# A graph attention kernel on one core: a shared PSUM bank listed whole, and a sorted table of places in the place of a scheduler

## The chip, the core and the metric

The kernel runs on one NeuronCore of a Trainium2 chip. Its engines are TensorE (PE in the profile, with its weight loads as PEld), VectorE (DVE), ScalarE (ACT), GpSimd (POOL) and SyncE (SP); each works through its own list of instructions in order and waits on semaphores. SyncE issues most transfers, GpSimd those that add into SBUF. The metric is the device time of one execution in microseconds (us); a change is told by the median of several.

## The reference, cut to what matters

A batch of 32 graphs of 512 nodes goes through two graph attention layers, behind a layer norm and with a residual sum around:

```python
def gat_layer(x, mask, W, a_src, a_dst, bias, concat):
    B, N, _ = x.shape
    H, F = a_src.shape
    xl = (x @ W).reshape(B, N, H, F)
    asrc = jnp.einsum('bnhf,hf->bnh', xl, a_src)
    adst = jnp.einsum('bnhf,hf->bnh', xl, a_dst)
    e = jax.nn.leaky_relu(asrc[:, :, None, :] + adst[:, None, :, :], NEG_SLOPE)
    e = jnp.where(mask[..., None], e, NEG_INF)
    attn = jax.nn.softmax(e, axis=1)
    out = jnp.einsum('bsdh,bshf->bdhf', attn, xl)
    if concat:
        out = out.reshape(B, N, H * F)
    else:
        out = out.mean(axis=2)
    return out + bias
mask = (adj > 0) | jnp.eye(N, dtype=bool)[None]
h = jax.nn.elu(gat_layer(h, mask, W1, att_src1, att_dst1, b1, concat=True))
h = gat_layer(h, mask, W2, att_src2, att_dst2, b2, concat=False)
...
h = jnp.maximum(_layernorm(x, axis=-1), 0.0)
x = x + _L0_gnn_ref(adj, h, ...)
```

`x` is 32 x 512 x 512 in float32 and `adj` int32. The first layer has 4 heads of 256 (W1 is 512 x 1024), the second one head of 512 (W2 is 1024 x 512). A float32 matmul shows as two passes in the trace, so `x2` in a list of instructions is `x4` there.

## The kernel before, in words

The kernel is written as a list of jobs. `Program.add` takes an engine, a cost, the keys that the job reads, those that it writes, and a function that emits its instructions; keys give the dependencies, so a key that is listed as written makes the job wait for every reader of it before. The helpers `act`, `dve`, `dma` (SyncE), `accumulate` (GpSimd, a transfer that adds) and `pe` add jobs. Where they record an instruction the profile gives their own line: L531 is every product, L514 every ScalarE operation, L517 every VectorE one, L520 every transfer of SyncE.

Graphs run in a pipeline. After a prologue (graph 0 whole, the projection of graph 1), 31 turns follow. A turn holds the second half of the first layer of one graph (`gather1`), the projection of a graph ahead (`project1`), the second layer of one behind (`project2`, `gather2`) and the preparations of the next (`load`, `norm`, `masks`). Products are Strassen's seven half products (`sevens`), numbered 1 to 7.

In the projection the product numbered 5 (`SMALL = (5,)`) is done by seven smaller ones of 128 x 129 columns, in `step`: a small block. There are two blocks in each of the 31 projections. The small products 2 and 3 go to the banks where the results are summed. The five others share one PSUM bank `tk`: 5 writes its upper half, key `tk + (1,)`, and 1, 6, 7 and 4 its lower half, key `tk + (0,)`. They run as 5, 1, 2, 6, 3, 7, 4. ScalarE copies the first two out: `f<-mm 128x129` is the copy of 5, `mm<-mm 128x129` that of 1 (and later of 4). VectorE adds 6 and 7 with `f`. In the trace and in the order, 5 is the first `mm<-wx,hx` of a block, 1 the `mm<-w_sb,hs 128x129` into the same bank, 2 the one into another bank, 6 the second `mm<-wx,hx`, 3 `mm<-w_sb,hx`, 7 `mm<-w_sb,hs` again, 4 `mm<-wx,hs`.

The scores of the softmax are spread over the partitions in `Soft.spread`: a VectorE transpose (`as<-z`), a 4 KB transfer out (`das<-as`) and a transfer in that repeats the rows (`as<-das`); the row maxima go the same way (`rr<-low`, `drr<-rr`, `rr<-drr`). ScalarE then works on `as` (`l<-as,z`), VectorE takes masked maxima (`l<-l,mt`), and later `p<-rr,z` on VectorE, a transfer that adds the mask (`p<-dm`, on GpSimd's queue) and the exponential (`p<-p,z`) on ScalarE make the attention matrix. The residual is loaded by `t<-in_x_dram`, stored by `out_dram<-t`. For graphs 0 and 1 the normed rows are transposed by TensorE with an identity matrix (`mm<-identf,x`, copied out as `ht<-mm`), for all others by a transfer.

What sets each engine's order is `Program.order`: it plays the program through with the costs, with latencies between engines (`PAIRS`, `CROSS`, `SAME`) and a model of the two DMA queues (`KIND`, `wires`). Whenever an engine is free in that play, it takes the ready job with the lowest rank. A rank is `PLACES[v] / 100` plus the length of a turn for each turn since the first. The emission follows that play.

## Time and profile before

| what | value |
| --- | --- |
| median of 3 runs | 2773.44 us (2768.58 to 2775.35) |
| profiled execution | 2769.33 us |
| its span | 2767.6 us |
| granted TensorE clock, mean | 0.999 |
| TensorE busy | 2742.4 us, 99% |
| VectorE busy | 2558.2 us, 92% |
| ScalarE busy | 2229.1 us, 81% |
| DMA | 502.14 MB, mean 181 GB/s |
| first product | 12.06 us after the start |

The span is the time from the first to the last record of the core; the time of an execution is a little longer. Times in the timeline count from the span's start. A row of the timeline reads: start, duration, engine, line, operation, what it writes and reads, shape, count, and in brackets the idle time before it with what ended it. Durations of matmuls include about 0.16 us in which the next one already runs. In the windows, the first number behind an engine is its busy time there, and PEclk the clock that TensorE was granted.

### The profile page before, as it was taken

How to read it: one execution, taken by the hardware profiler on the slowest of the kernel's cores; microseconds unless marked ns; L12 is line 12 of the kernel's file. 1: busy time of each engine (PE TensorE's matmuls, PEld its weight loads, DVE VectorE, ACT ScalarE, POOL GpSimd, SP SyncE). 2: the span in 40 equal slices, each digit the busy share in tenths (PEclk: the TensorE clock that was granted, in tenths of full speed). 3: DMA queues.
4: the chain of work that ended last, by engine and by line, in shares of the span. 5: the costliest groups of instructions: out<-in, count | busy, mean ns of one | idle time of the engine just before them, and what ended most of it. 6: DMA issues, size and time to landing. Idle time of an engine off the chain costs nothing. (4 is left out here: it accounts for less than half of the span.)

```text
span 2767.6 us, 42320 instructions
## 1 busy us (share of the span) xinstructions
PE 2742.4 (99%) x12924; PEld 2371.8 (86%) x12924; DVE 2558.2 (92%) x6732; ACT 2229.1 (81%) x4907; POOL 313.1 (11%) x356
## 2 busy tenths in 40 slices
PE   7999999999999999999999999999999999999999
PEld 6788888888888888888888888888888888888887
DVE  8999999999999999999999999999999999999996
ACT  5978888778887788877888877888778788788883
POOL 0110111101111111111011111111111111101110
PEclk9999999999999999999999999999999999999999
DMA  8657766667666667667676766766676767767563
GB/s 232 176 157 182 203 167 184 187 176 194 182 183 179 182 176 196 178 175 195 173 201 172 182 187 178 192 186 180 180 188 175 201 167 180 195 165 208 162 171 112
DMA packets 375864, 502.14 MB, mean 181 GB/s; under 512 B 222804, under 2 KB 227668, under 8 KB 375636
## 3 DMA queue, kind: packets, MB, share of 16 engines
q1 hardware_dynamic: 329844, 332.68, 42.4%
q0 software_dynamic: 45792, 166.74, 25.1%
q8 instruction: 103, 1.69, 0.3%
q14 instruction: 125, 1.02, 0.1%
HBM read 316.41 MB, written 51.31 MB: 133 GB/s over the span
## 5 line engine op out<-in xcount | busy, mean ns | idle before, releaser
L531 PE MATMUL mm<-w_sb,hs 128*128 128x257 f32 (+3 forms) x2908 | 667.0, 367 | 5.1 <-ACT mm L514 3.3
L531 PEld LDWEIGHTS mm<-w_sb,hs 128*128 128x128 f32 x2908 | 539.7, 190 | 87.7 <-ACT mm L514 6.7
L525 POOL DMA_DIRECT2D p<-dm x314 | 273.2, 875 | 2295.0 <-DVE p L517 764.3
L531 PE MATMUL mm<-w_sb,ht 128*128 128x258 f32 x2112 | 528.6, 382 | 2.7 <-ACT mm L514 2.5
L531 PE MATMUL mm<-p,xl 128*128 128x258 f32 (+1 forms) x1984 | 495.8, 383 | 0.1
L531 PE MATMUL mm<-w_sb,h 128*128 128x257 f32 x2056 | 477.8, 379 | 0.0
L517 DVE SCALAR_TENSOR_TENSOR p<-rr,z 128x512 f32<-128x512 f32 (+1 forms) x636 | 456.0, 742 | 2.4 <-DMA rr<-drr 2.4
L531 PEld LDWEIGHTS mm<-w_sb,ht 128*128 128x128 f32 x2112 | 393.7, 190 | 63.6 <-ACT mm L514 6.4
L514 ACT ACTIVATE p<-p,z 128x512 f32<-128x512 f32 (+1 forms) x636 | 433.4, 720 | 17.7 <-DVE p L517 12.4
L531 PEld LDWEIGHTS mm<-w_sb,h 128*128 128x128 f32 x2056 | 389.0, 189 | 58.4 <-ACT xl L514 0.5
L531 PEld LDWEIGHTS mm<-p,xl 128*128 128x128 f32 x1984 | 367.2, 190 | 52.7 <-issue 6.0
L514 ACT ACTIVATE mm<-mm 128x257 f32<-128x257 f32 (+2 forms) x498 | 169.8, 347 | 269.2 <-PE mm L531 236.2
L514 ACT ACTIVATE l<-as,z 128x512 f32<-128x512 f32 x516 | 354.4, 716 | 30.8 <-DMA as<-das 30.7
L514 ACT ACTIVATE l<-l,low 128x512 f32<-128x512 f32 x516 | 370.3, 721 | 7.6 <-DVE low L517 6.7
L517 DVE CUSTOM_DVE_ANT_1 l<-l,mt 128x512 f32<-128x512 f32 x516 | 346.2, 681 | 28.4 <-ACT l L514 27.4
L514 ACT ACTIVATE xl<-mm 128x258 f32<-128x258 f32 (+2 forms) x748 | 269.3, 382 | 91.4 <-PE mm L531 89.8
L514 ACT ACTIVATE h<-mm,b_sb 128x256 f32<-128x256 f32 (+1 forms) x504 | 231.0, 480 | 77.3 <-PE mm L531 76.6
L531 PE MATMUL mm<-t,hs 128*128 128x258 f32 (+1 forms) x992 | 246.1, 380 | 0.0
L517 DVE TENSOR_TENSOR xl<-xl,mm 128x258 f32<-128x258 f32 x372 | 155.3, 419 | 57.9 <-PE mm L531 48.3
L531 PEld LDWEIGHTS mm<-t,hs 128*128 128x128 f32 x992 | 185.8, 190 | 25.5 <-DVE t L517 0.2
L531 PE MATMUL mm<-xl,p 128*128 128x258 f32 (+2 forms) x752 | 189.7, 388 | 1.0 <-ACT h L514 0.6
L517 DVE SCALAR_TENSOR_TENSOR h<-xr,h 128x512 f32<-128x512 f32 x256 | 172.2, 683 | 6.1 <-ACT xr L514 6.1
(137 smaller groups left out, 3706.2 us busy)
## 6 DMA issues: line engine op xcount, KB each, us to landing
p<-dm POOLq DMA_DIRECT2D x314, 512.0 KB, 5.0
rr<-drr SPq DMA_DIRECT2D x159, 512.0 KB
x<-in_x_dram SPq DMA_DIRECT2D x129, 256.0 KB
adj<-in_adj_dram SPq DMA_DIRECT2D x128, 256.0 KB
as<-das SPq DMA_DIRECT2D x64, 512.0 KB
t<-in_x_dram SPq DMA_DIRECT2D x124, 256.0 KB
out_dram<-t SPq DMA_DIRECT2D x124, 256.0 KB
dm<-m SPq DMA_DIRECT2D x64, 256.0 KB
```

The lines of the kernel that those rows point to most:

```text
L514: prog.add("ACT", cost, reads, writes, lambda: nc.scalar.activation(*a, **k))
L517: prog.add("DVE", cost, reads, writes, lambda: f(*a, **k))
L525: lambda: nc.gpsimd.dma_start(to, at, accum_op=OP.add), size,
L531: f(*a, **k)
```

## The change

Every operation stays, in kind and number. Three things change.

First, each small product that goes into the shared bank is listed as writing both halves of it. Product 1 wrote only the lower half before and named the upper one as read, so it needed product 5 to be written and not copied. Now it waits for ScalarE's copy `f<-mm` of product 5. The other small products gain no wait.

Second, `order` doesn't play the program through any more. The table gives each job a place, in ten-thousandths of a microsecond; each engine's jobs are sorted by it, and the five lines are merged. The table's numbers are new, so every engine has another order. The latencies, the model of the queues and `LATE` are gone.

Third, the identity matrix has no tile of its own: it stands in a part of `hx` until the transposes of graphs 0 and 1 are done.

```diff
-LATE = {
-   
-}
...
-    CROSS, SAME = 0.15, 0.07
-    PAIRS = {("PE", "ACT"): 0.21, ("PE", "DVE"): 0.21, ("DVE", "POOL"): 0.58, ("POOL", "DVE"): 0.4}
-    AHEAD, MASK, OTHER = 3.5, (0.75, 1.84), 0.76
...
             if j < first:
-                v, i = j, 0
+                yield PLACES[j] / 10000
             elif j < last:
-                v, i = first + (j - first) % each, (j - first) // each + 1
+                yield PLACES[first + (j - first) % each] / 10000 + turn * ((j - first) // each + 1)
...
     def order(self):
-        jobs, rank = self.jobs, self.ranks()
-        n = len(jobs)
-        after = [[] for _ in range(n)]
+        jobs, rank, done = self.jobs, list(self.ranks()), []
+        after, left = [[] for _ in jobs], [len(job[2]) for job in jobs]
         for j, job in enumerate(jobs):
             for d in job[2]:
                 after[d].append(j)
...
+        lines = {e: [] for e in self.ENGINES}
+        for j in sorted(range(len(jobs)), key=lambda j: (rank[j], j)):
+            lines[jobs[j][0]].append(j)
+        lines = [deque(q) for q in lines.values()]
+        while any(lines):
+            q = min((q for q in lines if q and not left[q[0]]), key=lambda q: rank[q[0]])
+            j = q.popleft()
             done.append(j)
...
+            for k in after[j]:
+                left[k] -= 1
         return done
...
-    identf = sbuf.tile([P, P], F32, name="identf")
...
+    identf = hx[SMALL[0]][:, 0, :]
+    make_identity(nc, identf)
...
-                [xk], [pk], 0.44,
+                [xk, ("hx", SMALL[0])], [pk], 0.44,
...
             pe(
-                akeys + bkeys + ([tk + (1,)] if q == 1 else []), [bk], w / 576,
+                akeys + bkeys, [tk + (0,), tk + (1,)] if bk[:2] == tk else [bk], w / 576,
```

At the very start, SyncE now issues the four loads of `x` ahead of all weights, and VectorE finishes the statistics ahead of all sums of weights. TensorE runs 16 transposes ahead of its first product, 12 before.

**VectorE in the prologue, ahead of the sums of the second projection** (`hs<-ht` is the first of these sums, `ISA l` the masked maximum, `xr,part<-w_sb,t` a sum of weights, `z` score columns). Before:

```order
L517 TENSOR_TENSOR w_sb<-w_sb 128x1032
L517 COPY z_126<-mm_135 128x2
L517 TENSOR_SCALAR hs<-mm_133 128x256
L517 ISA l_99,low_129<-l_99,mt_110 128x512
L517 ISA low_129 128x1
L517 SCALAR_TENSOR_TENSOR xr_98,part<-w_sb,t_106 128x256
L517 SCALAR_TENSOR_TENSOR xr_97,part<-w_sb,t_106 128x256
L517 SCALAR_TENSOR_TENSOR xr_96,part<-w_sb,t_106 128x256
L517 COPY z_126<-mm_132 128x2
L517 ISA l_100,low_130<-l_100,mt_110 128x512
L517 ISA low_130 128x1
...
L517 ISA l_101,low_130<-l_101,mt_110 128x512
L517 ISA low_130 128x1
L517 TENSOR_TENSOR hs<-ht 128x512
```

And in the changed kernel:

```order
L472 COPY z_125<-mm_138 128x2
L472 ISA l_98,low_128<-l_98,mt_109 128x512
L472 ISA low_128 128x1
L472 COPY z_125<-mm_134 128x2
L472 COPY z_125<-mm_133 128x2
L472 BN_AGGR stats_122<-stats_122 128x2
L472 TENSOR_TENSOR m<-m,diag 128x2x128
L472 SCALAR_TENSOR_TENSOR xr_95,part<-w_sb,t_105 128x256
L472 STREAM_TRANSPOSE as_112<-z_125 128x32
L472 TENSOR_SCALAR z_125<-z_125 128x8
L472 TENSOR_TENSOR hs<-ht 128x512
```

Between the large `w_sb<-w_sb` and `hs<-ht` stood 20 rows with three maxima and three sums of weights; now there are 14, with one of each.

**SyncE in a turn, around the two spreads.** `t` is a residual load, `dm` and `mt` are mask transfers, `das` and `drr` the small transfers out. Before:

```order
L520 DMA adj_95<-in_adj_dram 128x512
L520 DMA t_109<-in_x_dram 128x512
L751 DMA_TRANSPOSE mt_110<-m 128x8x128
L520 DMA drr_118<-rr_114 4x8x32
L520 DMA dm_122<-m 128x1024
L520 DMA t_107<-in_x_dram 128x512
L520 DMA das_117<-as_113 4x8x32
L520 DMA rr_114<-drr_118 128x1024
L520 DMA as_113<-das_117 128x1024
```

And in the changed kernel:

```order
L475 DMA x_89<-in_x_dram 128x512
L475 DMA drr_117<-rr_113 4x8x32
L475 DMA dm_121<-m 128x1024
L475 DMA adj_93<-in_adj_dram 128x512
L706 DMA_TRANSPOSE mt_109<-m 128x8x128
L475 DMA das_116<-as_112 4x8x32
L475 DMA rr_113<-drr_117 128x1024
L475 DMA as_112<-das_116 128x1024
L475 DMA t_105<-in_x_dram 128x512
```

The residual loads stood ahead of and between the spreads' transfers; now the first comes behind `as<-das`, and the others follow.

**VectorE at the same place.** Before:

```order
L517 TENSOR_TENSOR xl_80<-xl_80 128x2x256
L517 SCALAR_TENSOR_TENSOR h_82<-xr_98,h_82 128x512
L517 BN_STATS stats_123<-x_89 128x6
L517 TENSOR_TENSOR t_106<-p_102 128x512
L517 TENSOR_SCALAR z_125<-xl 128x16
L517 TENSOR_TENSOR hs<-xl,hs 128x256
L517 STREAM_TRANSPOSE as_112<-z_125 128x32
```

And in the changed kernel:

```order
L472 TENSOR_TENSOR p_103<-p_103,t_106 128x2x256
L472 TENSOR_TENSOR xl<-xl,mm_137 128x258
L472 TENSOR_TENSOR xl_73<-xl_73 128x2x256
L472 TENSOR_SCALAR z_124<-xl 128x16
L472 STREAM_TRANSPOSE as_111<-z_124 128x32
```

The transpose that starts the spread of the scores now stands directly behind its `z`, and `z` behind `xl<-xl`.

**TensorE in a small block.** Before, in a turn:

```order
L531 MATMUL mm_132<-wx_85,hx_86 128x129
L531 MATMUL mm_132<-w_sb,hs 128x129
L531 MATMUL mm_136<-p_104,xl 128x256 x2
L531 MATMUL mm_134<-w_sb,hs 128x129
L531 MATMUL mm_132<-wx_85,hx_86 128x129
```

And in the changed kernel:

```order
L486 MATMUL mm_131<-wx_78,hx_79 128x129
L486 MATMUL mm_138<-w_sb,hs 128x258 x2
L486 MATMUL mm_131<-w_sb,hs 128x129
L486 MATMUL mm_135<-p_103,xl 128x256 x2
L486 MATMUL mm_133<-w_sb,hs 128x129
L486 MATMUL mm_131<-wx_78,hx_79 128x129
```

Product 1 stood right behind product 5; now a product of 258 columns in two steps stands between. Over the whole line there is one such product between them in 31 blocks, two in 30 (or as many columns of other products), and none in the very first block.

**ScalarE at that block.** Before:

```order
L514 ACTIVATE p_103<-p_103,z_126 128x512 x2
L514 ACTIVATE mm_134<-mm_132 128x129
L514 ACTIVATE f_92<-mm_132 128x129
L514 ACTIVATE xl<-mm_139 128x258
L514 ACTIVATE h_82<-mm_136,b_sb 128x256
```

And in the changed kernel:

```order
L469 ACTIVATE p_102<-p_102,z_125 128x512 x2
L469 ACTIVATE f_91<-mm_131 128x129
L469 ACTIVATE p_102<-p_102,z_125 128x512
L469 ACTIVATE mm_133<-mm_131 128x129
L469 ACTIVATE xl<-mm_138 128x258
```

The copy of product 5 moved ahead of that of product 1, and an exponential stands between them.

More of the change, by code (lines that the diff above doesn't have):

```diff
@@ L2 @@
 from contextlib import ExitStack
-from heapq import heappop, heappush
 import concourse.bass as bass
@@ L305, in order @@
                 after[d].append(j)
-        left = [len(job[2]) for job in jobs]
-        ready_at, self.start, done = [0.0] * n, [0.0] * n, []
-        free, soon, ready = dict.fromkeys(self.ENGINES, 0.0), defaultdict(list), defaultdict(list)
-        wires, now, behind = {"SP": deque(), "POOL": deque()}, 0.0, {"SP": 0.0, "POOL": 0.0}
-        for j in range(n):
-            if not left[j]:
-                heappush(soon[jobs[j][0]], (0.0, j))
-        def release(j, at):
-            for s in after[j]:
-                ready_at[s] = max(ready_at[s], at(s))
-                left[s] -= 1
-                if not left[s]:
-                    heappush(soon[jobs[s][0]], (ready_at[s], s))
@@ L468, in tile_gat @@
     hx = {n: sbuf.tile([P, 3, P], F32, name=f"hx{n}") for n in SMALL}
+    identf = hx[SMALL[0]][:, 0, :]
+    make_identity(nc, identf)
+    diag = sbuf.tile([P, P], BF16, name="diag")
+    nc.vector.tensor_scalar(diag, identf, -1.0, BIG, op0=OP.add, op1=OP.mult)
     rs = sbuf.tile([P, 2, 2, 2], F32, name="rs")
```

75 lines of the change are left out of this document (1 added, 74 removed), and 349 rows, old and new, of the table PLACES.

## The prediction

> **What bounds the kernel now.** I read first the page's totals, then the windows by stage, then the waits of TensorE and ScalarE, the length of a turn on TensorE's timeline, and last the chain and the timeline around the places where TensorE stands still. First the span and the busy times, from the page:
>
> ```profile
> span 2767.6 us, 42320 instructions
> PE 2742.4 (99%) x12924; PEld 2371.8 (86%) x12924; DVE 2558.2 (92%) x6732; ACT 2229.1 (81%) x4907; POOL 313.1 (11%) x356
> ```
>
> TensorE is busy for 2742.4 of 2767.6 us, and the change leaves every product as it is. So it can only move TensorE's 25 us of idle time, what its busy time hides (a late matmul stretches the one before it in a view that models ends), and a stretch at half clock. The windows by stage (columns: window, length, then busy time of PE, PEld, DVE, ACT, POOL, then the granted clock, the DMA share and GB/s; the second row is from a question of its own and lies between) say where:
>
> ```profile
> 12.00:57.00 45.00, 42.45 (x196) 36.40 (x197) 39.94 (x168) 25.46 (x58) 1.12 (x1) 0.96 0.94 271
> ...
> 57.00:400.00 343.00, 341.54 (x1555) 285.86 (x1555) 317.24 (x850) 290.83 (x633) 44.20 (x48) 1.00 0.66 173
> ...
> 400.00:2600.00 2200.00, 2195.71 (x10452) 1915.80 (x10451) 2058.63 (x5356) 1807.13 (x3987) 252.08 (x284) 1.00 0.69 183
> 2680.00:2767.00 87.00, 82.74 (x347) 64.36 (x345) 61.71 (x150) 35.85 (x78) 5.21 (x6) 1.00 0.45 134
> ```
>
> The steady stretch idles 4.29 us by this view. The turns show more. Here are the first small product of one block in four turns (start, duration):
>
> ```profile
> 403.97 0.39 PE L531 MATMUL mm<-wx,hx 128*128 128x129 f32 x2
> ...
> 573.87 0.39 PE L531 MATMUL mm<-wx,hx 128*128 128x129 f32 x2
> ...
> 658.57 0.39 PE L531 MATMUL mm<-wx,hx 128*128 128x129 f32 x2
> ...
> 2616.59 0.39 PE L531 MATMUL mm<-wx,hx 128*128 128x129 f32 x2
> ```
>
> 573.87 to 658.57 is one turn of 84.70 us. From 403.97 to 2616.59 there are 26 turns in 2212.62 us; 26 at 84.70 would be 2202.2. So 10.4 us are lost there, 0.4 a turn, and that is the largest sum in reach. Who is late there is in the waits of that stretch (engine, line, what it waited for: us in total, times, longest):
>
> ```profile
> PE mm L531 <- ACT mm L514: 4.0, 7, 1.2
> ...
> ACT l L514 <- DMA as<-das: 28.3, 31, 2.3
> ...
> ACT p L514 <- DMA p<-dm: 4.6, 7, 1.4
> ```
>
> TensorE waits for ScalarE's copies (`mm<-mm`), and ScalarE for two transfers: in every turn about 0.9 us for the spread scores `as<-das`, seven times for a mask sum `p<-dm`. One place of each kind. The chain (start, duration, what) goes through the mask sum:
>
> ```profile
> 2351.29 8.79 DMA p<-dm
> ...
> 2360.10 1.16 ACT p L514 x2
> ...
> 2361.34 0.27 ACT mm L514
> 2361.61 0.04 issue
> 2361.65 24.06 PE mm L531 x120
> ```
>
> The copy of a small product stands on ScalarE behind two exponentials whose mask came 8.79 us after its issue. The timeline at 843 to 855 has the spread:
>
> ```profile
> 840.41 0.65 DVE L517 TENSOR_TENSOR xl<-xl 128x512 f32<-128x512 f32 x1
> ...
> 842.90 1.23 SPq L520 DMA_DIRECT2D t<-in_x_dram  x1
> ...
> 843.19 0.21 DVE L517 STREAM_TRANSPOSE as<-z 128x32 f32<-128x32 f32 x1
> ...
> 844.24 0.52 SPq L520 DMA_DIRECT2D das<-as  x1
> ...
> 846.49 0.33 SPq L520 DMA_DIRECT2D as<-das  x1
> ...
> 852.53 1.95 ACT L514 ACTIVATE l<-as,z 128x512 f32<-128x512 f32 x3 [2.27 <-DMA as<-das]
> ...
> 854.38 0.52 ACT L514 ACTIVATE mm<-mm 128x129 f32<-128x129 f32 x2
> ...
> 854.69 1.14 PE L531 MATMUL mm<-w_sb,ht 128*128 128x258 f32 x4 [0.81 <-ACT mm L514]
> ```
>
> VectorE's transpose ends at 843.40, SyncE is in the issue of a residual load until 844.13, and the scores come to ScalarE at 852.53, 2.27 us late; the copies behind them stop TensorE for 0.81.
>
> **The change part by part: the new order in the turns.** The rows of the order give three shifts. On SyncE every residual load `t` stood before or between the transfers of the spread and now stands behind them: in the row above the issue of `t` held `das` back by 844.24 - 843.40 = 0.84 us. On VectorE the transpose `as<-z` now follows `xl<-xl` with only its `z` between; before, four other operations stood there too. The rows above give 843.19 - 840.41 = 2.78 us, of which the sum itself takes 0.65 and the small `z` about 0.1: some 2 us earlier at most, if `z` has what it needs. Against it stands that ScalarE's and TensorE's rows shift too. 0.84 plus a part of the 2 us covers the mean wait (28.3/31 = 0.9) and most of the worst (2.27). So I take the as-waits out and ScalarE is on time behind them. For the mask sums there is no such shift: the two exponentials and the copy stand about as far behind their issue as before, so I leave these, about 3 of the 10.4 us. Steady stretch: 10.4 - 3.4 = **-7 us**. Bounds: -10 if nothing is late any more, 0 if the lateness only moves (and a loss as in the second rival).
>
> **The added wait.** The product numbered 1 of each small block now waits for ScalarE's copy `f<-mm` of product 5 in the same bank's other half; there are 2 x 31 = 62. The timeline at 757 shows the four steps as they were:
>
> ```profile
> 757.66 0.39 PE L531 MATMUL mm<-wx,hx 128*128 128x129 f32 x2
> ...
> 757.86 0.47 ACT L514 ACTIVATE h<-mm,b_sb 128x256 f32<-128x256 f32 x1 [0.45 <-PE mm L531]
> 757.88 0.39 PE L531 MATMUL mm<-w_sb,hs 128*128 128x129 f32 x2
> ...
> 758.10 1.03 PE L531 MATMUL mm<-t,hs 128*128 128x258 f32 x4
> ...
> 758.30 0.28 ACT L514 ACTIVATE f<-mm 128x129 f32<-128x129 f32 x1
> ```
>
> Product 5 takes the array 757.88 - 757.66 = 0.22 us. A copy starts about 0.20 us after the product before it has left the array (758.30 against 758.10), takes 0.28, and TensorE starts 0.04 after such a copy (2361.61 to 2361.65 in the chain). So product 1 could start 0.22 + 0.20 + 0.28 + 0.04 = 0.74 us behind product 5. In the new order a product of 258 columns in two steps stands between in 31 blocks, two such products in 30, none in the very first. One takes 0.87 us (a run of four passes, 1.03, less the pipeline's 0.16), so in the 31 product 1 stands at 0.22 + 0.87 = 1.09: 0.35 us to spare if ScalarE is free by then; in the 30 it is 1.2 us. ScalarE's line was changed with it: `f<-mm` now comes ahead of the other copy, with one exponential between. Cost 0, hidden under those products, but for the first block, 0.74 - 0.22 = 0.5 us; what it costs with the cover gone is the second rival. VectorE's sums wait for products 6 and 7 as before.
>
> **The beginning.** Rows of the timeline:
>
> ```profile
> 10.16 0.43 DVE L517 SCALAR_TENSOR_TENSOR xr<-w_sb,p 128x256 f32<-128x256 f32 x1 [0.93 <-DMA w_sb<-in_L_gnn_W_dram]
> ...
> 11.00 0.16 DVE L517 SCALAR_TENSOR_TENSOR stats<-stats 128x4 f32<-128x4 f32 x1
> ...
> 12.06 2.82 PE L531 MATMUL mm<-identf,x 128*128 128x128 f32 x12 [12.06 <-ACT x L514]
> ...
> 14.67 5.92 PE L531 MATMUL mm<-w_sb,ht 128*128 128x258 f32 x24
> ...
> 47.86 0.69 DVE L517 TENSOR_TENSOR hs<-ht 128x512 f32<-128x512 f32 x1
> ...
> 49.40 1.65 PE L531 MATMUL mm<-w_sb,hs 128*128 128x258 f32 x4 [1.32 <-DVE hs L517]
> ```
>
> Before, the statistic at 11.00 stood behind two sums of weights, the first at 10.16 late by its load; now it stands ahead of all, the loads of `x` go first, and 16 transposes instead of 12 run before the first product. The four moved ones are (14.67 - 12.06)/12 x 4 = 0.87 us; they are gained if TensorE starts that much earlier, and 11.00 - 10.16 = 0.84 us lie in VectorE's two sums. I take **-0.7**, bounds 0 and -1.5 (the sums and the moved transposes do not add, but an earlier load might). Around 47, VectorE has `hs<-ht` in line behind masked maxima, weight sums and statistics. From the large weight sum to `hs<-ht` there stood 20 rows, among them three maxima and three sums of weights; now there are 14, with one maximum and one sum. Two maxima, 0.68 us each by the page's row of their group (below), and two sums of about 0.4 by the row at 10.16 are 2.2 us, more than the 1.32 that TensorE stood; ScalarE's copy of the last `ht` then decides. What that stall brought with it stands in windows of this stretch:
>
> ```profile
> 46.40:49.90 3.50, 1.66 (x7) 1.15 (x7) 3.50 (x13) 3.48 (x12) 0.00 (x0) 1.00 1.02 351
> 49.90:53.30 3.40, 3.40 (x11) 2.86 (x11) 3.04 (x11) 2.36 (x8) 0.00 (x0) 0.50 0.86 213
> ```
>
> ```profile
> L517 DVE CUSTOM_DVE_ANT_1 l<-l,mt 128x512 f32<-128x512 f32 x516 | 346.2, 681 | 28.4 <-ACT l L514 27.4
> ```
>
> After 3.5 us with TensorE busy for 1.66, the granted clock was 0.50 for 3.4 us, which cost 1.7 us of work. I take 1.0 for the stall and the 1.7, less the 0.5 of the first block's added wait: **-2.2**, bounds +2 (another stall at the same price) and -5 (all of it). [...]
>
> **The first turns, the end, the tile.** At 57 to 400 us TensorE idles 1.46 us; the new order lengthens no row there, but what the prologue lent to the first turn is also used up earlier, and I add **+0.5** (bounds -1.5 and +3, the size of the stalls at 47 to 50). The end idles 4.26 of 87 us: **-0.6**, bounds -2 and +1, as its last chain is matmuls to 2763.9. The identity in the place of a tile of its own makes VectorE's first `hx` wait for the last transposes, which `hs<-ht` ahead of it needs anyway: 0. Fewer waits on SyncE and more on the others cost their engines' queue nothing that the profile shows: 0.
>
> Sum: -0.7 - 2.2 + 0.5 - 7 - 0.6 = -10.0 against the profiled execution's 2769.3 (span 2767.6 and 1.7 around it): **2759.3 us**. The median of the runs shown, 2773.4, is 4.1 above that execution; their 2768.6 to 2775.4 I read as stalls that differ from run to run. With half of these gone too, the median could stand some 2 above the sum, and a little more gained would take that back; I keep 2759.3.
>
> **Rivals.** *The lateness only moves.* The transfers share one set of DMA engines, busy for 0.69 of the stretch; a residual load that goes later meets a mask sum, and 8.79 us as in the chain comes as often as before. For it: seven waits for `p<-dm` that the new order does not touch. Against: the wait for `as<-das` comes every turn and has its cause in the row. Then only the beginning and the end gain: 2769.3 - 0.7 - 2.2 - 0.6 + 0.5 = 2766.3, to 2770 with the median run's 4.1 on it; 0.18.
>
> *The added wait isn't covered.* ScalarE reaches `f<-mm` late, because the two exponentials ahead of it in its new line, 1.16 in the chain's row, are still to run when product 5 is done. Then product 1 waits 1.16 - 0.35 = 0.81 us in the 31 blocks with the smaller cover and not in the 30 others: 31 x 0.81 = 25 us, 2759.3 + 25 = 2784. It decides from (2781.8 - 2759.3)/31 = 0.73 us a block, ScalarE 1.1 us late in each; below that it only eats the gain. For it: ScalarE is late by 0.9 in each turn now. Against: that lateness lies at another place of the turn, and in the row at 757.86 ScalarE idled 0.45 right ahead of these copies. 0.13, the slower side.
>
> *The half clock comes again* though the stall is shorter, by a mechanism that any short pause in that stretch sets off: 2759.3 + 1.7 = 2761.0; 0.05. [...]
>
> **How the numbers follow.** The forecast has 0.64, the half clock 0.05: faster 0.69; moved lateness: same 0.18; slower 0.13. 0.3% of the time, 8.3 us, is about what a measurement of this kernel can tell from no change: faster is below 2765.1, slower above 2781.8. The low end, 2749, has every term at its better bound (-1.5 - 5 - 1.5 - 10 - 2 = -20); the high end, 2774, takes in the moved lateness and 3 us of the runs' spread. Left out are the uncovered wait and the rest of the tails.
>
> **What would show it.** Right: first transposes near 11.4, no half clock at 50, `ACT l <- DMA as<-das` well under 28 us, 26 turns near 2205, waits of TensorE for `mm` no more than the three or four of the mask sum. Wrong: TensorE waiting for ScalarE's `f` before product 1 in most blocks (turns over 85.1), or for VectorE's sums; loads of `x` or masks that land later than their users; a first turn with a stall of several us.

## The result, and the profile after

| | before | changed |
|---|---|---|
| median (lowest to highest), us, 12 runs each | 2770.3 (2765.9 to 2775.4) | 2774.3 (2770.7 to 2781.6) |
| profiled execution, us | 2769.3 | 2770.7 |
| its span, us | 2767.6 | 2769.0 |
| start of the first matmul (a transpose), us | 12.06 | 10.28 |
| one turn with nothing late, us | 84.70 | 84.82 |
| 26 turns, us | 2212.6 | 2213.5 |

The changed kernel takes 1.0019 times as long, 95% interval 1.0011 to 1.0026: 0.2% slower. The interval lies clear of 1, but the size is within the 0.3% that the prediction called no change; the median is 15 us above the forecast. The profiled execution was the fastest of its twelve.

The page's totals and the windows by stage of the changed kernel (window, length, busy time of PE, PEld, DVE, ACT and POOL, granted clock, DMA share, GB/s):

```profile
span 2769.0 us, 42322 instructions
...
PE 2743.4 (99%) x12924; PEld 2373.1 (86%) x12924; DVE 2570.4 (93%) x6732; ACT 2237.4 (81%) x4907; POOL 323.3 (12%) x356
```

```profile
12.00:57.00 45.00, 42.94 (x209) 36.47 (x208) 41.82 (x176) 25.64 (x61) 1.12 (x1) 1.00 0.86 259
...
57.00:400.00 343.00, 339.97 (x1548) 284.99 (x1547) 319.41 (x849) 291.18 (x631) 44.32 (x48) 1.00 0.67 177
400.00:2600.00 2200.00, 2196.13 (x10445) 1917.28 (x10444) 2065.37 (x5347) 1813.85 (x3985) 262.20 (x284) 1.00 0.68 183
...
2680.00:2767.00 87.00, 83.46 (x348) 64.62 (x346) 64.22 (x152) 36.26 (x79) 4.34 (x5) 1.00 0.43 131
```

The granted clock of the prologue is 1.00 now (0.96 before). From 57 to 400 us TensorE is busy for 1.6 us less, and the steady stretch is as it was to half a microsecond. The turns say more; the starts of the same product as in the prediction, the first and the last of 26 turns and two neighbours between (start, duration):

```profile
400.83 0.39 PE L486 MATMUL mm<-wx,hx 128*128 128x129 f32 x2
...
1593.32 0.39 PE L486 MATMUL mm<-wx,hx 128*128 128x129 f32 x2
...
1678.14 0.39 PE L486 MATMUL mm<-wx,hx 128*128 128x129 f32 x2
...
2614.31 0.39 PE L486 MATMUL mm<-wx,hx 128*128 128x129 f32 x2
```

An undisturbed turn takes 1678.14 - 1593.32 = 84.82 us where it took 84.70, and 26 of them 2213.48 where they took 2212.62. So 26 x 0.12 = 3.1 us are a small new loss in every turn, and what single turns lose beyond that fell only from 10.4 to 2213.48 - 26 x 84.82 = 8.2 us. The waits in that stretch show where (engine, line, waited for: us, times, longest):

```profile
ACT l L469 <- DMA as<-das: 47.5, 30, 2.7
...
ACT p L469 <- DMA p<-dm: 8.8, 11, 1.9
...
PE mm L486 <- ACT f L469: 3.0, 5, 1.5
```

Before, these rows were 28.3 for the spread scores, 4.6 for the mask sums, and TensorE's largest wait was 4.0 for `mm`. Now ScalarE waits longer for both transfers; TensorE waits for the copy `f`. The timeline of the turn with the longest of these waits shows how. `p<-dm` is the fourth mask sum of the turn, SPq is SyncE's queue; in brackets the idle time ahead and what ended it:

```profile
989.62 0.40 SPq L475 DMA_DIRECT2D rr<-drr  x1
990.12 0.44 SPq L475 DMA_DIRECT2D adj<-in_adj_dram  x1
990.48 0.86 POOL L480 DMA_DIRECT2D p<-dm  x1 [2.79 <-PE mm L486]
...
996.48 0.39 PE L486 MATMUL mm<-wx,hx 128*128 128x129 f32 x2
...
998.33 0.72 ACT L469 ACTIVATE p<-p,z 128x512 f32<-128x512 f32 x1 [1.88 <-DMA p<-dm]
998.96 0.26 ACT L469 ACTIVATE f<-mm 128x129 f32<-128x129 f32 x1
...
999.27 0.49 PE L486 MATMUL mm<-w_sb,hs 128*128 128x129 f32 x2 [1.54 <-ACT f L469]
```

Here SyncE issues two loads of 512 and 256 KB (`rr<-drr`, the spread minima, and `adj`) just ahead of the mask sum's issue on GpSimd. The sum is late, ScalarE stands 1.88 us for it, `f<-mm` stands in line behind that exponential, and product 1 of the small block behind `f`: TensorE stands still for 1.54 us. This turn (turn 7 of the 26, counted from 0) is a special one: GpSimd issues the sum 2 us later than in the others, 6.0 us ahead of product 5 instead of 8.1. It does so once, in turn 7, in the kernel before too (6.5 instead of 8.4); why is not shown. In the other turns the two loads follow the sum, as in turn 5:

```profile
818.30 0.86 POOL L480 DMA_DIRECT2D p<-dm  x1 [0.72 <-PE mm L486]
...
819.50 0.39 SPq L475 DMA_DIRECT2D rr<-drr  x1
819.99 0.41 SPq L475 DMA_DIRECT2D adj<-in_adj_dram  x1
```

`rr` is issued 1.2 us behind the sum and `adj` 1.7; in the kernel before it was 5.6 and 1.1 in most turns. So it is `rr` above all that came near. In the packet records of the DMA engines the fourth sum's median time from issue to its last packet is 7.3 us over the 26 turns, 6.3 before; in the turns 0, 6, 12, 18 and 24, and in turn 8 behind the special one, it is 8.0 to 8.6. TensorE's stalls at this place are 5.0 us in all, 1.8 of them in turn 7; before they were 3.7, with 1.5 in turn 7.

To see where the 1.4 us between the two profiled executions come from, I counted for each pair of neighbouring matmuls the time between their starts beyond 0.84 ns a column, which is what they take where nothing stands between them (258 columns every 0.217 us, as in the eight from 2563.57 to 2565.31 us of the changed kernel), where it is more than 0.01 us:

| stretch | before | changed | difference | forecast |
|---|---|---|---|---|
| up to the first matmul | 12.06 | 10.28 | -1.8 | -0.7 with the next row |
| from there to 30 us | 1.9 | 2.2 | +0.4 | |
| 30 to 57 us, half clock included | 5.5 | 3.1 | -2.4 | -2.2 |
| 57 to 400 us | 2.6 | 4.1 | +1.5 | +0.5 |
| 400 to 2600 us | 10.0 | 11.5 | +1.5 | -7.0 |
| 2600 us to the last matmul | 2.8 | 4.3 | +1.5 | -0.6 with the next row |
| behind the last matmul | 3.7 | 4.5 | +0.8 | |

The rows add up to +1.5. The beginning gave what was forecast; the steady stretch did not, and three other places took the gain back.

### The profile page after: what moved, and what is told of

The parts are those of the page before. It is cut to its first block, busy times and chain, and to the rows that moved or that the text cites. A ratio compares the mean times of both kernels' runs of the same rounds, so it can differ in the third digit from the quotient of the medians.

```text
span 2769.0 us, 42322 instructions
## 1 busy us (share of the span) xinstructions
PE 2743.4 (99%) x12924; PEld 2373.1 (86%) x12924; DVE 2570.4 (93%) x6732; ACT 2237.4 (81%) x4907; POOL 323.3 (12%) x356
## 5 line engine op out<-in xcount | busy, mean ns | idle before, releaser
L486 PE MATMUL mm<-w_sb,ht 128*128 128x258 f32 x2112 | 517.5, 381 | 2.0 <-ACT ht L469 1.2
L469 ACT ACTIVATE p<-p,z 128x512 f32<-128x512 f32 (+1 forms) x636 | 444.7, 716 | 19.9 <-DMA p<-dm 12.9
L469 ACT ACTIVATE l<-as,z 128x512 f32<-128x512 f32 x516 | 356.3, 715 | 54.3 <-DMA as<-das 51.8
L469 ACT ACTIVATE h<-mm,b_sb 128x256 f32<-128x256 f32 (+1 forms) x504 | 222.7, 475 | 58.7 <-PE mm L486 56.8
L486 PE MATMUL mm<-xl,p 128*128 128x258 f32 (+3 forms) x752 | 190.1, 389 | 0.2 <-ACT h L469 0.2
L472 DVE TENSOR_TENSOR xl<-xl,mm 128x258 f32<-128x258 f32 x372 | 147.3, 416 | 43.8 <-PE mm L486 43.3
```

The source lines that it names most:

```text
L469: prog.add("ACT", cost, reads, writes, lambda: nc.scalar.activation(*a, **k))
L472: prog.add("DVE", cost, reads, writes, lambda: f(*a, **k))
L486: f(*a, **k)
```

## The experiments

The first four set out from two explanations. A: the mask sum of each turn now shares the DMA engines with `rr` and `adj`, which the new order issues close to it. B: the wait added by the new listing is what costs, a stall here and a little in each turn. The runs come from several chips. The ratio behind a time, with its 95% interval, is to the kernel before on the same chip; the changed kernel's own ratio is 1.0019, and runs are compared by these ratios.

**The old listing with the new table.** Every engine's order is the same, word for word; only what product 1 waits for is as before.

```diff
-                akeys + bkeys, [tk + (0,), tk + (1,)] if bk[:2] == tk else [bk], w / 576,
+                akeys + bkeys + ([tk + (1,)] if q == 1 else []), [bk], w / 576,
```

> The new table with the old listing of the keys: every engine's order is word for word that of the changed kernel, and only the wait of product 1 for the copy of product 5 is gone from the 61 blocks that have it. Theory A (the loss lies in late mask sums: the exponentials ahead of both copies on ScalarE come late, and product 1 merely is the first to feel it): product 2 then stands still in the place of product 1, in the same turns, a little shorter since it stands 1.1 us further on; 1 to 2 us less than the changed kernel's 2774.3. Rival B (the added wait itself is the loss): the stalls at the small blocks go, about 5 us less, at or below the kernel before.

Measured: 2808.1 us, 1.0154 [1.0140, 1.0168]: (1.0154 - 1.0019) x 2767 = 37 us slower than the changed kernel, which neither explanation had. TensorE's largest wait, its wait for `f` (3.4 us in the changed kernel), and ScalarE's ahead of `f` (20.0 us there):

```profile
PE mm L486 <- ACT mm L469: 29.2, 34, 1.0
...
PE mm L486 <- ACT f L469: 3.9, 6, 2.1
...
ACT f L469 <- PE mm L486: 79.0, 31, 2.7
```

and the second small block of one turn of this kernel:

```profile
846.53 0.39 PE L486 MATMUL mm<-wx,hx 128*128 128x129 f32 x2
846.75 1.91 PE L486 MATMUL mm<-w_sb,ht 128*128 128x258 f32 x8
848.49 0.39 PE L486 MATMUL mm<-w_sb,hs 128*128 128x129 f32 x2
...
848.91 0.28 ACT L469 ACTIVATE f<-mm 128x129 f32<-128x129 f32 x1 [2.66 <-PE mm L486]
...
850.38 0.26 ACT L469 ACTIVATE mm<-mm 128x129 f32<-128x129 f32 x1
...
850.70 0.49 PE L486 MATMUL mm<-w_sb,hs 128*128 128x129 f32 x2 [0.96 <-ACT mm L469]
```

Product 5 is done at 846.75, but its copy `f` starts at 848.91, 0.20 after product 1 (848.49) has left the array. So here the copy of product 5 waits for product 1, though they use different halves of the bank. In the first small block of a turn `f` comes first as in the changed kernel, and where it is late product 1 stands for it even with the old listing (the row of 3.9 us). Both fit a bank that is kept as one in either kernel, where the one that comes first in the merged order goes first; the merged order itself is not shown. In the second block the new listing puts product 1 behind the copy, and the old one puts the copy behind product 1. In the new order those two stand 2 us apart there, and the old listing then makes the copy late by as much in each turn. The changed kernel has the copy 0.20 behind product 5's end:

```profile
837.56 0.39 PE L486 MATMUL mm<-wx,hx 128*128 128x129 f32 x2
...
837.98 0.28 ACT L469 ACTIVATE f<-mm 128x129 f32<-128x129 f32 x1 [0.69 <-PE mm L486]
...
839.52 0.39 PE L486 MATMUL mm<-w_sb,hs 128*128 128x129 f32 x2
```

So the edit did not take the wait away, as it was meant to: it turned it round in the second blocks and left it in the first ones. It does not test B. Against B stands that in most blocks product 1 comes long after the copy's end (839.52 against 838.26), and a run below in which the stalls go with the new listing in place.

**The new listing in the kernel before.** The same line the other way round, with the old table and the program played through as before.

> The kernel before with the whole bank listed and nothing else; its planner plays the program with that dependency and gives another order. Theory A: the planner covers the wait as it covers others, so within 2 us of the kernel before. Rival B: 4 us or more slower than before, with waits of TensorE for the copy f in many turns.

Measured: 3114.5 us, 1.1262 [1.1247, 1.1277]. The largest waits of TensorE:

```profile
PE mm L531 <- ACT mm L514: 51.3, 68, 4.0
PE mm L531 <- ACT ht L514: 45.0, 13, 9.4
```

TensorE's wait for `f` makes 11.8 us, in 12 places. Playing the program through with other dependencies changes every engine's line. That doesn't price the wait: it says that listing and table can't be judged apart from each other.

**Less traffic.** The result stores of the changed kernel write a quarter of their columns, so three quarters of the output are left out.

```diff
-                dma(STORE, [xk, xk + (0,), xk + (1,)], (), out[b, d * P : (d + 1) * P, :], xt)
+                dma(STORE, [xk, xk + (0,), xk + (1,)], (), out[b, d * P : (d + 1) * P, : D // 4], xt[:, : D // 4])
```

> The changed kernel, but the result's stores take only a quarter of their columns (so most of the output is left out): 24 of 502 MB less traffic, order and waits as they were. If the late mask sums come from the DMA engines being shared (theory A), ScalarE's wait for p<-dm falls from 12.9 us to less than half, and the stalls at the first small block of a turn (about 5 us in the profile) with it: 3 to 5 us faster than the changed kernel. If the mask sum is late because GpSimd issues it late (rival C), nothing changes there.

Measured: 2771.8 us, 1.0021 [1.0011, 1.0030], as the changed kernel. ScalarE's wait for `p<-dm` fell from 12.9 to 9.4 us, not to less than half, and TensorE's stalls at the first small block stayed (5.2 us against 5.0); the fourth sum's median is 7.3 us as in the changed kernel. So the stores don't make the sum late. They are 24 of 502 MB, so this says little of the general load, and it does not tell A from a sum that is issued late.

**`rr` and `adj` behind the spread.** In the changed kernel these two transfers go behind `as<-das` on SyncE, in all turns but the last; all other engines keep their order.

```diff
+SHIFT = {1497: 8.81, 1248: 4.41}
...
-                yield PLACES[first + (j - first) % each] / 10000 + turn * ((j - first) // each + 1)
+                yield PLACES[first + (j - first) % each] / 10000 + turn * ((j - first) // each + 1) + (SHIFT.get(first + (j - first) % each, 0) if j < last - each else 0)
```

> The changed kernel with two transfers moved on SyncE in every turn but the last: the spread-in of the maxima (rr<-drr, 512 KB) and one mask load (adj, 256 KB) go behind the spread-in of the scores (as<-das), and no longer just ahead of and behind the issue of a turn's fourth mask sum. Theory A (the sum is late because it shares the DMA engines with these two): the fourth sum lands about 6 us after its issue and not 7.2, ScalarE's wait for p<-dm falls below 4 us, the stalls at the first small block (4.3 us with 0.7 behind them) go, and it is 4 to 5 us faster than the changed kernel. Rival C (the sum is late because it is issued late, or queues behind the third): no change. Rival D: the maxima then come late to VectorE: slower.

Measured: 2769.7 us, 1.0006 [0.9997, 1.0015]; against the changed kernel's 1.0019 [1.0011, 1.0026] that is 0.0013 x 2768 = 3.6 us faster, with intervals that touch. The waits of ScalarE and of TensorE (12.9 and 3.4 before the edit):

```profile
ACT p L469 <- DMA p<-dm: 6.6, 6, 2.6
```

```profile
PE mm L486 <- ACT f L469: 0.4, 1, 0.4
```

Turn 7 in this kernel, where GpSimd again issues the sum late (6.1 us ahead of product 5), with the two transfers where they stand now:

```profile
992.14 0.86 POOL L480 DMA_DIRECT2D p<-dm  x1 [2.68 <-PE mm L486]
994.18 0.33 SPq L475 DMA_DIRECT2D as<-das  x1
994.60 0.44 SPq L475 DMA_DIRECT2D rr<-drr  x1
995.13 0.41 SPq L475 DMA_DIRECT2D adj<-in_adj_dram  x1
...
998.25 0.39 PE L486 MATMUL mm<-wx,hx 128*128 128x129 f32 x2
...
998.74 0.27 ACT L469 ACTIVATE f<-mm 128x129 f32<-128x129 f32 x1
```

By the packet records this sum takes 3.9 us, where it took 7.5 in turn 7 of the changed kernel, and the copy `f` starts 0.27 behind its product's end. Over the 26 turns the median is 5.9 us instead of 7.3, with the issue as far ahead of product 5 as before (8.1 us). That answers the rival of a late issue: it is there in one turn, and costs nothing once the loads are away. TensorE's stalls at the first small block go from 5.0 us to 0.05, and they are 0 in the run with both edits below. Six profiles with the loads in their changed place and the same order in these turns have 3.4 to 8.0 us there. So A holds for the stalls. Its worth in time is less sure: by the six profiles the 26 turns take 2210.6 to 2218.3 us, and here 2210.4. What single turns lose is 5.0 us here and 8.2 in the changed kernel; an undisturbed turn still takes 84.82. Which of the two loads does it, this run can't tell; that they do it by sharing the DMA engines is argued, not shown.

**The copies ahead of the exponentials.** ScalarE's two copies of the first small block go ahead of the exponentials that wait for the mask sum, so that a late sum can't stop TensorE.

```diff
+PLACES[1267] -= 9050; PLACES[1269] -= 5540
```

> The changed kernel with two copies moved on ScalarE, in the first small block of each turn: the copy of product 5 goes ahead of the exponential that waits for the fourth mask sum, and the copy of product 1 ahead of the one behind it. The sum is as late as before. Theory A (TensorE stands only because the copies queue behind a late exponential): ScalarE's wait for p<-dm stays near 12 us, TensorE's wait for f goes and one of about 0.5 us for the other copy is left in the late turns: 3 us faster than the changed kernel. If ScalarE loses more by waiting for product 5 in every turn: no faster.

Measured: 2789.0 us, 1.0082 [1.0069, 1.0096]. TensorE's wait for `f` is gone (0.4 us, once), and so is most of ScalarE's wait for the sum (4.4 us). But the exponentials now come behind the copies, and TensorE loses 0.1 to 0.3 us at four places of that block in every turn, 16 us in all over the 26. What it waits for there is not shown. Lateness that a few turns have is cheaper than a line that is a little late in all of them.

**Two small swaps.** ScalarE's copy of a 256-column product goes ahead of `xr<-h` in each turn, where an undisturbed turn loses 0.09 us; and in the first turn VectorE's two sums `xl` go ahead of the masked maximum, which stood 3.2 us in line for ScalarE.

```diff
+PLACES[1359] -= 2305; PLACES[1123] = 2016100; PLACES[1121] = 2016120
```

> The changed kernel with two swaps that have nothing to do with transfers: in each turn ScalarE's copy of a product to a second bank (mm<-mm 128x256) goes ahead of an exponential for elu (xr<-h), and in the first turn two of VectorE's sums xl<-xl,mm go ahead of a masked maximum that waits for ScalarE. Expected: the 0.09 us that TensorE loses in every turn at that place goes (26 x 0.09 = 2.3 us in the steady stretch, 2.7 in all), and the 2.9 us stall near 213 us shrinks to under 1: together 4 to 5 us faster than the changed kernel.

Measured: 2771.4 us, 1.0017 [1.0008, 1.0026], no gain that can be told from the changed kernel. In its profile an undisturbed turn takes 84.74 instead of 84.82, so that 2.1 us of the 3.1 are found; but single turns lost 11.0 us instead of 8.2 in this execution. In the first turn TensorE's wait for `xl`, 2.9, gave place to one of 1.4 for ScalarE's exponential and one of 0.9 for a copy 5.6 us later.

**Both.** The edits of the last run and of the one that moves `rr` and `adj` together.

> The moves of the kernels e4 and e6 together. If both causes stand and add: 8 to 10 us faster than the changed kernel, 2764 to 2766 us, and faster than the kernel before by some 3 us or more. If the late sums only move elsewhere: 4 to 5 us.

Measured: 2767.8 us, 1.0006 [0.9997, 1.0015]: the time of the kernel before, and no better. That is the second outcome, 4 us; the two swaps add nothing that shows.

**The residual loads ahead of the spread again.** Two of the residual loads `t`, which the change moved behind the spread's transfers on SyncE, go ahead of them again.

```diff
+SHIFT = {1499: -2.58, 1498: -4.04}
```

(The numbers are rounded; the ranks add them as in the run that moved `rr` and `adj`.)

> The changed kernel with two of a turn's four residual loads (t) put back ahead of the spread of the scores on SyncE, where the old order had them; nothing else moves. The prediction's step says that these loads make the scores late and TensorE stand: then ScalarE waits 1 to 2 us for as<-das at that spread in each turn, which it does not in the changed kernel, TensorE stands behind it again, and 3 us or more are lost. Rival: the scores come late, but what is behind them on ScalarE has room in the new order; then the wait shows on ScalarE and the time moves by less than 2 us.

Measured: 2949.2 us, 1.0650 [1.0634, 1.0666]. The waits of ScalarE for the spread, of TensorE, and of SyncE's queue:

```profile
ACT l L469 <- DMA as<-das: 192.8, 57, 6.3
```

```profile
PE mm L486 <- DVE h L472: 86.7, 27, 4.1
```

```profile
SPq L475 <- PE mm L486: 213.2, 62, 5.0
```

ScalarE's wait for the spread was 51.8 in the changed kernel, and that of SyncE's queue for TensorE's products 203.4. That the loads stand in SyncE's line for the last reader of their buffer, with the spread behind them, is my reading of the order; the row of the queue alone, 213.2 against 203.4, does not show it. So that the loads stand behind the spread is worth much in the new order, but the price is far above the 0.84 us a turn of the kernel before, where such a load was issued within 1.23 us (the row at 842.90). The mean granted clock was 0.974 in this run (1.000 in the changed kernel): by it (1 - 0.974) x 2948.5 = 77 us of full clock were not granted, and I put about 77 of the 175 us lost down to that, an estimate. This run says that the place matters; it does not give the size of the forecast's term.

**The identity in a tile of its own**, as in the kernel before.

```diff
-    identf = hx[SMALL[0]][:, 0, :]
+    identf = sbuf.tile([P, P], F32, name="identf")
```

> The changed kernel with the identity matrix in a tile of its own again. Expected: nothing, within 1 us of the changed kernel, with the same waits in the first 60 us.

Measured: 2774.6 us, 1.0029 [1.0019, 1.0039]; the interval overlaps that of the changed kernel, so no effect shows.

**Three places for the spread.** The DRAM places of the scores and minima, three instead of two, since the lateness of every sixth turn looked like two and three buffers falling together.

```diff
-    das = slots("das", 2, [2 * NT, P], F32, dram)
-    drs = slots("drr", 2, [2 * NT, P], F32, dram)
+    das = slots("das", 3, [2 * NT, P], F32, dram)
+    drs = slots("drr", 3, [2 * NT, P], F32, dram)
```

> The changed kernel with three places in DRAM for each of the small spread transfers (das, drr) instead of two. In the changed kernel the fourth mask sum lands after 7.1 to 7.4 us in most turns and after 8.0 to 8.6 in every sixth (turns 0, 6, 12, 18, 24 of the steady stretch), whose buffers repeat with a period of six turns: three for masks and attention matrices, two for the spread. If the DRAM places of the spread make that period, it becomes three turns, or the long ones go; if not, every sixth stays long.

Measured: 2777.7 us, 1.0034 [1.0019, 1.0049]. The fourth sum still lands 7.8 to 8.7 us behind its issue in the same five turns. In this profile turn 9 is late too (8.9). It isn't these places; what makes the period of six stays open.

**The stall of the beginning put back.** In the changed kernel, sums of weights go ahead of `hs<-ht` on VectorE: four in the first run, eight in the second.

```diff
+PLACES[388] = 64590; PLACES[390] = 64591; PLACES[392] = 64592; PLACES[393] = 64593
```

```diff
+PLACES[388] = 64590; PLACES[390] = 64591; PLACES[392] = 64592; PLACES[393] = 64593; PLACES[395] = 64594; PLACES[398] = 64595; PLACES[391] = 64596; PLACES[396] = 64597
```

> The changed kernel with one stall put back in the beginning: on VectorE four sums of weights (0.41 us each in the trace, 0.35 apart) go ahead of the half sum hs<-ht at 44.67, so that this stands some 1.4 us later; its product started 0.2 us behind it, so TensorE should stand still for about 1.2 us at 46 to 48, about as long as it did in the kernel before (1.32). All other engines' order is the same. If the half clock of the kernel before hung on that stall, the granted clock falls to 0.5 for about 3.4 us again and the head of the program is 1.2 + 1.7 = 2.9 us longer. If it hung on something else that the change took away (other loads, other work of the engines), the clock stays at 1.00 and only the 1.2 us are lost. [...]

> The same with eight sums of weights ahead of hs<-ht: 2.8 us later, TensorE stands still for about 2.6 us. [...] Head 2.6 us longer, 4.3 with the half clock.

Measured: 2771.9 and 2776.9 us, one execution each, with spans of 2770.1 and 2775.1 (2769.0 without the stall). The stall with four sums:

```profile
48.46 1.14 PE L486 MATMUL mm<-w_sb,hs 128*128 128x258 f32 x4 [0.83 <-DVE hs L472]
```

and with eight:

```profile
48.76 2.09 PE L486 MATMUL mm<-w_sb,hs 128*128 128x258 f32 x4 [2.44 <-DVE hs L472]
```

The first stall is shorter than the expected 1.2 us, because TensorE came to it later in that execution (its row ahead starts at 46.49 instead of 45.34). With 0.83 us of standing still the clock stays at 1.00. With 2.44 it is 0.50 from 48.50 to 55.32, and by the count above TensorE loses 4.7 us more between 30 and 57 us than in the changed kernel, near the 4.3 expected. So a stall put back at that place brought the half clock back when it was 2.44 us long, and not at 0.83; for the kernel before, with 0.53 and 1.32, this speaks for the stall as the cause.

It does not hang on the stall's length alone. The table takes a stretch of about 3.4 us around a stall, as long as the half clock of the kernel before lasted (49.88 to 53.29 us, 3.41), and the granted clock in the stretch behind it. The "first turn" is the stall at 216.38 that a later row of this document shows.

| execution and stall, us | stretch | TensorE busy in it, us | stretch behind it | granted clock there |
|---|---|---|---|---|
| before: 0.53 and 1.32 | 46.47 to 49.88 | 1.62 | 49.88 to 53.29 | 0.50 |
| four sums: 0.83 | 46.40 to 49.90 | 2.50 | 49.90 to 53.30 | 1.00 |
| eight sums: 2.44 | 45.30 to 48.80 | 1.06 | 48.80 to 52.20 | 0.50 |
| changed, first turn: 2.86 | 214.50 to 217.91 | 1.53 | 217.91 to 221.32 | 1.00 |

Behind the longest of these stalls, 2.86 us, the clock stayed at 1.00, and behind two of 1.85 us together it was 0.50. TensorE's work in the stretch does not tell them apart either: 1.53 us in the first case and 1.62 in the second. The run with four sums has the stall of 2.9 us in its first turn too, and a mean granted clock of 1.000, which has no room for the 1.7 us of a half clock. What else decides is not shown.

## Why the prediction was wrong

The sum had -10.0 and the profiled execution has +1.5. Of these 11.5 us, 8.5 lie in the steady stretch: "So I take the as-waits out and ScalarE is on time behind them ... Steady stretch: 10.4 - 3.4 = -7 us" is the step that failed. By place, the 26 turns gained 3.5 us at the spread, lost 1.3 more at the mask sums, which the sum had at nothing, and lost 3.1 by a new loss in every turn, which it did not have. That makes the 0.9 us by which they got longer.

- **The beginning, -0.7 and -2.2: right for the profiled executions, in part by luck.** The first product starts 1.8 us earlier, of which the next 20 us take 0.4 back. `hs<-ht` is on time, the half clock behind it is gone, and the run that put a stall of 2.44 us back had a half clock there again. That the kernel before paid 1.7 for it was in part chance: of 54 other executions of that kernel 36 have a mean granted clock of 1.000 and 18 of 0.999. I read a mean of 0.999 as at least one half clock of 3.41 us, an estimate from two profiles: the one of the kernel before, with one, has 0.9993, that of the changed kernel, with none up to its last matmul, 0.9998. The added wait of the first block, taken as 0.5, is the 0.42 of this row:

```profile
48.00 0.49 PE L486 MATMUL mm<-w_sb,hs 128*128 128x129 f32 x2 [0.42 <-ACT f L469]
```

- **The added wait elsewhere, 0: right in its size.** The cover holds wherever the mask sum is on time. The working was wrong in one point: it took product 1 and the copy `f` as free of each other before. In the rows at 757.88 and 758.30 the copy started 0.20 after product 1 had left the array; there ScalarE was itself busy with `h` until 758.33. In the block at 163 it was idle, and the copy started 0.20 after product 1's end (163.32) all the same:

```profile
163.09 0.39 PE L531 MATMUL mm<-w_sb,hs 128*128 128x129 f32 x2
...
163.52 0.28 ACT L514 ACTIVATE f<-mm 128x129 f32<-128x129 f32 x1 [0.34 <-PE mm L531]
```

  So the change did not add a wait to a block that had none, it turned one round. The rival with the uncovered wait had the right chain (late exponentials, then `f`, then product 1) but as a thing of 31 blocks; it came in seven of the 26 turns, where a mask sum was late.

- **The spread, the main part of -7: the mechanism right, the size wrong.** At this place of the turn, the one that the prediction read at 853, ScalarE waited 24.1 us for the scores in the 26 turns and now waits 2.5; in the turn shown the scores are there when it comes:

```profile
841.47 0.53 SPq L475 DMA_DIRECT2D das<-as  x1
...
843.90 0.33 SPq L475 DMA_DIRECT2D as<-das  x1
...
849.03 1.94 ACT L469 ACTIVATE l<-as,z 128x512 f32<-128x512 f32 x3
```

  With that the stalls of TensorE behind this spread are gone. By the count of gaps they had been 3.5 us in the 26 turns, though, not 7: the 28.3 us that ScalarE waited were mostly slack, and I had given TensorE's 10.4 us to the two kinds of lateness by a guess at shares. "Well under 28 us" for that row failed outright, at 47.5: the other spread of the turn makes 45.1 of it, 4.1 before, and no stall of TensorE stands behind it.

- **"For the mask sums there is no such shift ... I leave these": failed too.** I looked at the lines of ScalarE and GpSimd and not at what else SyncE issues at that moment. `rr` came from 5.6 to 1.2 us behind the fourth sum's issue, its landing went from 6.3 to 7.3 us, its issue stands 8.1 us ahead of product 5 instead of 8.4, and TensorE's stalls went from 3.7 to 5.0 us by the count. Moving `rr` and `adj` away took these stalls out; in time that was 3.6 us, with intervals that touch. The rival "the lateness only moves" named the mechanism (a load that comes to stand at another place meets a mask sum), with another load than the ones that did it, and 2766 to 2770 as its time.

- **Not in the sum at all: 0.12 us in each turn.** About 0.09 of it stands at ScalarE's copy of a 256-column product behind `xr<-h`, which the swap found; the rest is spread over single products of 0.06 and less. No row of the kernel before could show it; a line that is 0.12 us late 26 times is 3.1 us, most of the 3.8 that the beginning gained.

- **The first turns and the end, +0.5 and -0.6: wrong by 1 and 3 us.** In the first turn VectorE's masked maximum stands in line for ScalarE ahead of two sums that TensorE needs:

```profile
214.36 0.69 DVE L472 CUSTOM_DVE_ANT_1 l<-l,mt 128x512 f32<-128x512 f32 x1 [3.19 <-ACT l L469]
...
215.58 0.74 DVE L472 TENSOR_TENSOR xl<-xl,mm 128x257 f32<-128x257 f32 x2
...
216.38 1.14 PE L486 MATMUL mm<-t,hs 128*128 128x258 f32 x4 [2.86 <-DVE xl L472]
```

  That is 2.9 us at one place; the row as a whole is +1.5, within the bound of +3 given for it. In the profiled execution the clock stayed at 1.00 behind this stall (217.91 to 221.32 us). In seven of the experiments' profiles the wait for `xl` is 2.9 us as well; the mean granted clock is 1.000 in two of them and 0.999 or less in five, which does not say where it was lower. In one of the five, with the old listing, it was 1.00 from 215 to 400 us. A half clock of 3.41 us, as in the kernel before, costs 1.7. The end lost 1.5 before its last matmul and 0.8 behind it. I have no experiment on the end.

With -1.4, -2.4, +1.5, +1.5 and +2.3 in place of -0.7, -2.2, +0.5, -7 and -0.6 the sum is +1.5. That goes by the profiled execution. The median of the twelve lies another 3.6 us above it, 0.3 above the high end of the range. Part of it is the half clock: ten of the twelve executions have a mean granted clock of 0.999 or less, and the profiled one is not among them. So, by that reading of the means, most executions of the changed kernel do pay for a half clock, perhaps in the first turn, which would be the third rival's mechanism at another place and is not shown, and the profiled execution was lucky. In the two profiles this counts 1.7 us for the change, in a typical pair of executions 1.7 against it; that swing of 3.4 is enough for the 2.6 us by which the medians lie further apart (4.0) than the profiled executions (1.4). This is an estimate from the mean clocks, as no second execution of the changed kernel itself was profiled.

## What to carry to other kernels

When an order moves a transfer, look at every queue for what is now issued within a few microseconds of it: here two loads on SyncE, issued within 2 us of a mask sum on GpSimd's queue, made it land 1.4 us later than with them away, and that went through two engines to TensorE. A wait on an engine off the critical path is worth only what TensorE itself lost behind it (3.5 of 28 us here), so count the stalls of the bounding engine place by place before you promise the sum. And a listing of dependencies and a table of places belong together: the new table with the old listing cost 1.4% against the changed kernel, the old table with the new listing 12.6% against the kernel before. And one profile of each kernel is little when the effect is 3 us and executions of the same order differ by 8: ask whether a stall at one place comes back in other profiles before pricing it.

## What the runs showed of the hardware

- A mask sum's transfer of 512 KB took 7.3 us from issue to its last packet (median of 26, changed kernel) with 768 KB of loads issued 1.2 and 1.7 us behind it on another queue, and 5.9 in the run with these moved further back. In the one turn in which they were issued ahead of it, it took 7.5, against 3.9 with them behind. With the result stores cut to a quarter the median was 7.3 too, and the stalls 5.2 us against 5.0.
- With two residual loads moved ahead of a spread on SyncE, ScalarE waited 192.8 us for the spread in place of 51.8, and the run lost (1.0650 - 1.0019) x 2767 = 175 us in all, of which about 77 go with its mean granted clock of 0.974 (an estimate from that mean).
- The granted clock of TensorE was 0.50 for 3.41 us in the kernel before, behind 3.41 us with TensorE busy for 1.62; with a stall of 2.44 us put back it was 0.50 from 48.50 to 55.32, and with one of 0.83 it stayed at 1.00. Behind the stall of 2.86 us in the changed kernel's first turn, with TensorE busy for 1.53 of 3.41 us, it stayed at 1.00. What decides is not shown.
- The fourth mask sum was late (8.0 to 8.6 us) in every sixth turn of the changed kernel, turns 0, 6, 12, 18 and 24, and with three DRAM places for the spread in place of two it took 7.8 to 8.7 us in the same five. So these places don't make the period, and its cause is open.
